# Two-layer transformer on one core: another order for row 3's band values, the first expert blocks and the fetched results in the last stage

## The chip, the cores and the metric

The kernel runs as one program on 1 core of one Trainium2 chip. The metric is the device time of that core in microseconds (us). TensorE is called PE (and PEld for its weight loads), VectorE DVE, ScalarE ACT, GpSimd POOL and SyncE SP. Each engine works through a queue of its own in order; a semaphore holds an engine at an instruction until what it needs is there.

## The reference

There are 4 rows of 512 tokens with 128 channels, all in float32. Each of two layers adds an attention and an expert layer to its input, both reading the same layer norm:

```
x = x + attn0(norm(x)) + experts0(norm(x))   # band attention, 16 heads, window 64; 16 experts, top 4
xn = norm(x)
x = x + attn1(xn) + experts1(xn)             # full attention, 16 heads of 8; 8 experts, top 2

# attn0: logits of the window's 64 pairs from two gelu forms of disp_win - disp;
#        weights = softmax(logits); out = weights @ val_win; out @ W_cproj
# attn1: softmax(q k^T / sqrt(128)) v, then @ w_out
# experts1: score = relu(x rw1 + rb1) rw2 + rb2; gate = softmax over the two best
#        out = sum over experts of gate_e * (relu(x W1_e + b1_e) W2_e + b2_e),  128 -> 512 -> 128
```

The change touches the end of `attn0` for the last row and everything of layer 1.

## The kernel before, in words

**Two stages.** Layer 0 takes the rows one after the other and lasts to about 845 us of the span. The last stage, from there to the end, weaves two tracks: the whole attention of layer 1, and everything else that is left. `weave` and `woven` take at each turn a step from the track whose next step, as a share of the number given with it, is least. A generator's `yield` ends one turn. This decides the order in which the program is written; a scheduler then places each instruction in its engine's queue, with waits as the data needs them. Instructions under `tc.high_priority(offset=FIRST)`, the attention's scores, maxima, exponentials and products, are placed ahead of others.

**Attention.** `full_attention` works on 16 groups (4 rows by 4 groups of 4 heads) in 128 steps. Each step has 8 score matmuls as the profile counts them (L1205). In the first 6 steps both halves serve row maxima (`nmax`, DVE, L1222), in the following 116 one half serves maxima and one exponentials (`ex`, ACT, L1229), since the maxima run 12 pairs ahead, and in the last 6 both serve exponentials. Between steps PE does `weigh` (the products with the values, L1117), `queries` and `keys`, and `columns` (transposes, L1053) into the only buffer of `abank`. `with_maxima` turns a group's maxima and adds them to the queries (`qa`, DVE, L1108); the exponentials' scores of that group need it. `normalise` turns a group's sums and divides (`rd` and `o`, DVE, L1131 and L1132). `turned` (L1141), `project_out` (L1147) and `add_rows` (L287) end a row, and `done` writes the row to the output once attention and experts have both added to it.

**Row 3's band values.** The last row's `attn0` is not yet ended when the last stage begins. ACT makes the weights e (L850), which go to memory as `by_t`. `band_values` then goes through four tiles of tokens: load `f` from `by_t` (L317), turn it on PE (L326) and copy it on ACT (L327) to `g`, store that as `by_s`, load it back with a slant as `wb`, and multiply with the values (L358). `begin` follows (layer norm, `xs`, the router), then `in_order_of_experts`, which sorts the tokens into blocks of one expert each. All this is the generator `row3`.

**Experts.** Blocks hold 128 pairs of a token and its expert. `early` has the 31 blocks of rows 0 to 2, `last_row` the 15 of row 3. `experts(m, pool, deep)` fetches the weights `wx` and rows `xb` by indirect DMA on POOL (L581), turns the rows (L604, copied at L606), and multiplies twice: the first half L637 with its four activations (three on ACT at L650, one on DVE at L648), the second half L611 with its bias on DVE (`y`, L618) and the store to `ys` (SP, L619). The halves' PSUM comes from `bank`, which has two buffers; `y` has one. `paced` keeps the halves in their place between the attention's steps.

**Results.** `results(m, lag)` fetches, a round, two tiles' rows of `ys` (`got`, four fetches on POOL) and adds the fetched rows with their gates to x, `lag` rounds later (L676, DVE). `behind` ties the first of a round's fetches to the attention's pace, and with lag over 1 also the first sum of each even tile.

**The last stage's second track.** Before, `row3` and the first 36 turns of the early experts are woven, then come the rest of the early experts, then `results(early, 2)` woven with the last row's experts, and then `results(last_row, 1)`.

Of the kernel before, what the change touches and what calls it, by code (L numbers as in the profile page):

```python
# [30 lines left out]
B, T, C = 4, 512, 128  # L31
# [66 lines left out]
def woven(*tracks):  # L98


    live = [[g, n, 0] for g, n in tracks]
    while live:
        t = min(live, key=lambda v: (v[2] + 1) / v[1])
        t[2] += 1
        if next(t[0], "end") == "end" or t[2] == t[1]:
            live.remove(t)
        yield


def weave(*tracks):  # L110
    for _ in woven(*tracks):
        pass
# [3 lines left out]
def two_layers(ctx: ExitStack, tc: tile.TileContext, w: dict, consts: bass.AP, out: bass.AP):  # L116
# [8 lines left out]
    def bank():  # L125
        return ps_f.tile([P, 512], FP, tag="f", name="bank")
# [17 lines left out]
    def c_(name):  # L144
        return cst[:, offs[name][0]:offs[name][1]]
# [92 lines left out]
    def transposed(src):  # L238

        pt = bank()  # L240
        for i in range(TPB):
            nc.tensor.transpose(pt[:, i * P:(i + 1) * P], src[:, i, :], ident)
        return pt
# [46 lines left out]
    chain = ctx.enter_context(tc.tile_pool(name="chain", bufs=2))  # L290
# [130 lines left out]
    early, last_row = Pairs(range(B - 1)), Pairs(range(B - 1, B))  # L421
# [11 lines left out]
    def begin(b, pool, tag):  # L433

        m = part_of[b]
        at = (b - m.rows[0]) * TPB
        own = slice(at, at + TPB)
        xn = chain.tile([P, TPB, C], FP, tag="o", name="xn", bufs=1)
        rw1 = pool.tile([C, F1], FP, tag=tag, name="rw1")
        nc.sync.dma_start(out=rw1, in_=w["L1_ffn_rw1"])  # L440
        layernorm(b, xn)
        nc.sync.dma_start(
            out=m.xs[at * P:(at + TPB) * P, :].rearrange("(t p) c -> p t c", p=P), in_=xn
        )
        yield
        pt = transposed(xn)
        nc.scalar.copy(xT[:, b * T:(b + 1) * T], pt)
        yield
        hs = []
        for c in range(4):  # L450
            ph = bank()
            paced(nc.tensor.matmul(ph, rw1[:, c * P:(c + 1) * P], xT[:, b * T:(b + 1) * T], start=True, stop=True))
            h = chain.tile([P, T], FP, tag="h", name="h", bufs=4)
            nc.scalar.activation(h, ph, AF.Relu, bias=cols[:, c:c + 1])
            hs.append(h)
            if c % 2:
                yield
        pg = bank()
        for i in range(TPB):
            for c in range(4):  # L460
                nc.tensor.matmul(
                    pg[:, i * E1:(i + 1) * E1], hs[c][:, i * P:(i + 1) * P], rw2[:, c, :],
                    start=(c == 0), stop=(c == 3),
                )
        scores = small.tile([P, TPB, E1], FP, tag="scores1", name="scores1")
        nc.vector.tensor_tensor(
            scores, pg[:, :TPB * E1].rearrange("p (t e) -> p t e", e=E1),
            rb2[:, None, :].to_broadcast([P, TPB, E1]), ALU.add,
        )
        routes(  # L470
            small, "pairs", scores, E1, K1, c_("lead8"), m.gates[:, own, :], m.picks[:, own, :]
        )
        yield
# [111 lines left out]
    def experts(m, pool, deep):  # L585

        NS, NB, xs, ys = m.tiles, m.blocks, m.xs, m.ys
        wx, xb, xbT = {}, {}, {}

        def weights(j):  # L590
            wx[j] = pool.tile([P, WX], FP, tag="wx", name="wx", bufs=deep)
            fetch(wx[j], w["pair_weights"], m.which[:, j:j + 1])

        def load(g):
            k = min(2, NB - 2 * g)
            xb[g] = pool.tile([P, 2, C], FP, tag="xb", name="xb", bufs=2)
            for i in range(k):
                fetch(xb[g][:, i, :], xs[:, :], m.whose[:, 2 * g + i:2 * g + i + 1])

        def turn(g):  # L600
            k = min(2, NB - 2 * g)
            pt = bank()
            for i in range(k):
                nc.tensor.transpose(pt[:, i * P:(i + 1) * P], xb[g][:, i, :], ident)  # L604
            xbT[g] = pool.tile([C, 2 * P], FP, tag="xbT", name="xbT", bufs=2)
            nc.scalar.copy(xbT[g][:, 0:k * P], pt[:, 0:k * P])  # L606

        def second(j, h):
            py = bank()
            for c in range(4):  # L610
                mm = nc.tensor.matmul(  # L611
                    py[:, 0:C], h[:, c * P:(c + 1) * P], wx[j][:, F1 + c * P:F1 + (c + 1) * P],
                    start=(c == 0), stop=(c == 3),
                )
                own = own + [mm] if c else [mm]
            paced(own[0], own[-1])
            y = pool.tile([P, C], FP, tag="y", name="y")
            nc.vector.tensor_tensor(y, py[:, 0:C], wx[j][:, 2 * F1 + 4:WX], ALU.add)  # L618
            nc.sync.dma_start(out=ys[j * P:(j + 1) * P, :], in_=y)  # L619

        for j in range(deep):
            weights(j)
        load(0)
        yield
        load(1)
        turn(0)
        yield
        late = None
        for j in range(NB):
            g = j // 2  # L630
            if j % 2 and 2 * (g + 1) < NB:
                turn(g + 1)
                if 2 * (g + 2) < NB:
                    load(g + 2)
            ph = bank()
            for c in range(4):
                mm = nc.tensor.matmul(  # L637
                    ph[:, c * P:(c + 1) * P], wx[j][:, c * P:(c + 1) * P],
                    xbT[g][:, j % 2 * P:(j % 2 + 1) * P], start=True, stop=True,
                )  # L640
                own = own + [mm] if c else [mm]
            paced(own[0], own[-1])
            h = pool.tile([P, T], FP, tag="h", name="h", bufs=2)
            for c in range(4):
                b1 = wx[j][:, 2 * F1 + c:2 * F1 + c + 1]
                to = h[:, c * P:(c + 1) * P]
                if c == 3:
                    nc.vector.tensor_scalar(to, ph[:, c * P:(c + 1) * P], b1, 0.0, ALU.add, ALU.max)  # L648
                else:
                    nc.scalar.activation(to, ph[:, c * P:(c + 1) * P], AF.Relu, bias=b1)  # L650
            yield
            if late:
                second(*late)
            late = (j, h)
            if j and j - 1 + deep < NB:
                weights(j - 1 + deep)
            yield
        second(*late)
        yield

    def results(m, lag):

        got = {}
        for g in range(m.tiles // 2 + lag):
            if g < m.tiles // 2:
                got[g] = chain.tile([P, 2, 2, C], FP, tag="h", name="got", bufs=4)
                for i in range(2):
                    for k in range(2):
                        ins = fetch(got[g][:, i, k, :], m.ys[:, :], m.place[:, k, 2 * g + i:2 * g + i + 1])
                        if not i and not k:  # L670
                            behind(ins)
            if g >= lag:
                for t in range(2 * (g - lag), 2 * (g - lag) + 2):
                    x = x1[:, m.rows[0] * TPB + t, :]
                    for k in range(2):
                        ins = nc.vector.scalar_tensor_tensor(  # L676
                            x, got[g - lag][:, t % 2, k, :], m.gate[:, k, t:t + 1], x, ALU.mult, ALU.add
                        )
                        if not t % 2 and not k and lag > 1:
                            behind(ins)  # L680
                    if t % TPB == TPB - 1:
                        done(m.rows[0] + t // TPB)
            yield

    def after(*parts):
        for p in parts:
            yield from p


    with ExitStack() as l0:  # L690
        prep = l0.enter_context(tc.tile_pool(name="prep", bufs=1))
# [32 lines left out]
        ready = {}  # L724
# [237 lines left out]
        pq = l0.enter_context(tc.tile_pool(name="begin0", bufs=1))  # L962
# [67 lines left out]
    def full_attention():  # L1030
# [163 lines left out]
        for t in range(min(todo), max(todo) + 1):  # L1194
# [37 lines left out]
            yield  # L1232

    pq = ctx1.enter_context(tc.tile_pool(name="experts", bufs=1))
    first_experts = experts(early, pq, 3)
    row3 = after(band_values(B - 1, ready[B - 1][1]), begin(B - 1, chain, "valn"), in_order_of_experts(last_row, pq, pq, "tb"))
    weave(
        (full_attention(), 142),
        (after(
            woven((row3, 32), (first_experts, 36)), first_experts,  # L1240
            woven((results(early, 2), 9), (experts(last_row, pq, 3), 34)), results(last_row, 1),
        ), 32 + 66 + 9 + 34 + 3 + 10),
    )


# [40 lines left out]
```

## Time and profile before

| | us |
|---|---|
| median of three timed runs | 1317.91 |
| lowest and highest of them | 1314.45 and 1323.61 |
| the profiled execution's own time | 1310.25 |
| its span, first to last instruction | 1308.1 |
| busy in the span: PE, DVE, ACT, POOL | 1027.7, 1010.7, 955.3, 139.1 |
| start of attention step 1, 6, 119 | 870.5, 891.35, 1269.55 |
| DVE's sums L676 waiting for `got`, 15 times in all | 27.8 |
| PE's L326 waiting for `f`, once | 16.8 |
| mean granted clock of PE | 0.903 |

The profile is of one execution. In its rows the start or the busy time comes first, then the mean length of one, engine and line of the kernel, the operation with its output and input, and in brackets the idle time before it and what ended that. A busy share over the whole span mixes layer 0, which lives on DVE and ACT, with the last stage, which lives on PE. So the last stage is read from views cut to its own stretch of time.

### The profile page before, as it was taken

Reading aid. Unit: us, or ns where it says so; the run is one execution under the profiler, and the core shown is the slowest. Engines: PE = TensorE matmul, PEld = TensorE weight load, DVE = VectorE, ACT = ScalarE, POOL = GpSimd, SP = SyncE. Lnnn points to the kernel's source line nnn. Section 1 sums busy time; section 2 is a strip of 40 time slices with the busy share of each in tenths; the row PEclk is TensorE's granted clock in tenths of the full one; section 3 lists DMA queues with packets and bytes.
Section 4 is the critical chain, followed back from the end, with each engine's and each line's share of the span. In section 5 each row is a group of like instructions: output and inputs, shape, how many; then the busy total and the mean of one; then the engine's idle time right before and its main releaser. Section 6 shows DMA issues by size and latency. Waiting matters only on the chain. (4 is left out here: it accounts for less than half of the span.)

```text
span 1308.1 us, 18393 instructions
## 1 busy us (share of the span) xinstructions
PE 1027.7 (79%) x7029; PEld 463.6 (35%) x7029; DVE 1010.7 (77%) x1246; ACT 955.3 (73%) x1154; POOL 139.1 (11%) x165
## 2 busy tenths in 40 slices
PE   5677876778796677897577886739898999978996
PEld 3232333223342132443222342414344545534442
DVE  5999999999988999998999979625355475545552
ACT  5999998999987899898899987224454445534454
POOL 3000000000000000000000000231121123234512
PEclk9898898889998799898788988759999999989999
DMA  7221213347212445311355411154632324532431
GB/s 272 65 85 43 73 55 131 84 117 181 57 46 79 116 105 144 99 57 32 123 131 143 122 51 29 63 164 124 169 93 94 97 66 123 144 104 90 122 112 37
DMA packets 161969, 132.17 MB, mean 101 GB/s; under 512 B 68101, under 2 KB 142266, under 8 KB 160346
## 3 DMA queue, kind: packets, MB, share of 16 engines
q1 hardware_dynamic: 151290, 91.72, 25.7%
q0 software_dynamic: 10304, 38.64, 9.5%
q8 instruction: 56, 0.92, 0.3%
q10 hardware_dynamic: 288, 0.64, 0.1%
q14 instruction: 31, 0.25, 0.1%
HBM read 97.93 MB, written 33.03 MB: 100 GB/s over the span
## 5 line engine op out<-in xcount | busy, mean ns | idle before, releaser
L790 DVE TENSOR_TENSOR z<-proj 128x2044 f32<-128x2044 f32 (+31 forms) x256 | 547.8, 2161 | 14.3 <-PE lbank L804 10.1
L804 PE MATMUL lbank<-z,place 128*32 128x504 f32 (+18 forms) x2048 | 302.5, 669 | 135.2 <-ACT z L796 73.4
L796 ACT ACTIVATE z<-z,posb 128x1024 f32<-128x1024 f32 (+31 forms) x256 | 264.3, 1100 | 24.3 <-DVE z L790 23.6
L792 ACT ACTIVATE z<-z,brep 128x2048 f32<-128x2048 f32 (+31 forms) x128 | 240.8, 1913 | 13.7 <-DVE z L790 11.2
L1229 ACT ACTIVATE ex<-score 128x1024 f32<-128x1024 f32 x128 | 130.4, 1024 | 160.7 <-PE score L1205 160.7
L1222 DVE TENSOR_REDUCE nmax<-score 128x2 f32<-128x1024 f32 x128 | 156.1, 1224 | 84.6 <-PE score L1205 84.2
L804 PEld LDWEIGHTS lbank<-z,place 128*32 128x32 f32 x2048 | 45.3, 115 | 288.9 <-ACT z L796 150.7
L1205 PE MATMUL score<-kpad,qpad 32*128 32x512 f32 x384 | 111.4, 652 | 19.4 <-DVE nmax L1222 14.1
L581 POOL DMA_INDIRECT wx<-pair_weights,which x46 | 43.5, 946 | 663.9 <-PE abank L1097 432.4
L1205 PE MATMUL score<-qa,kpad 32*128 32x512 f32 x384 | 104.1, 654 | 2.9 <-ACT ex L1229 2.8
L893 PE MATMUL accbank<-wT,lin 128*128 128x128 f32 x512 | 84.8, 308 | 23.7 <-DVE lin L891 23.6
L893 PEld LDWEIGHTS accbank<-wT,lin 128*128 128x128 f32 x512 | 71.9, 210 | 75.3 <-DVE lin L891 39.1
L906 PE MATMUL gbank<-tT,wT 128*128 128x512 f32 x128 | 73.3, 656 | 27.1 <-DMA wT<-wT_all 21.2
L648 DVE TENSOR_SCALAR h<-bank,wx 128x128 f32<-128x128 f32 x46 | 16.0, 349 | 77.9 <-ACT h L650 77.9
L913 PE MATMUL gbank<-tT,wT 128*128 128x512 f32 x128 | 69.3, 624 | 4.5 <-ACT glu L909 4.5
L1117 PE MATMUL accbank<-ex,vaug 128*32 128x512 f32 x512 | 71.1, 621 | 0.2 <-ACT ex L1229 0.2
L650 ACT ACTIVATE h<-bank,wx 128x128 f32<-128x128 f32 x138 | 40.7, 365 | 39.2 <-PE bank L637 39.1
L637 PE MATMUL bank<-xbT,wx 128*128 128x128 f32 x368 | 53.9, 291 | 4.3 <-DVE y L618 3.5
L637 PEld LDWEIGHTS bank<-xbT,wx 128*128 128x128 f32 x368 | 47.4, 201 | 24.3 <-issue 15.1
L611 PEld LDWEIGHTS bank<-wx,h 128*128 128x128 f32 x368 | 46.6, 197 | 21.5 <-issue 19.0
L611 PE MATMUL bank<-wx,h 128*128 128x128 f32 x368 | 53.4, 289 | 0.8 <-ACT g L327 0.6
L909 ACT ACTIVATE glu<-gbank,gbt 128x512 f32<-128x512 f32 x64 | 44.2, 690 | 9.0 <-PE gbank L906 6.4
(242 smaller groups left out, 1379.8 us busy)
## 6 DMA issues: line engine op xcount, KB each, us to landing
r<-route SPq DMA_DIRECT2D x64, 256.0 KB
wb<-by_s SPq DMA_DIRECT2D x32, 512.0 KB
wT<-wT_all SPq DMA_DIRECT2D x48, 192.0 KB
by_t<-e SPq DMA_DIRECT2D x8, 1024.0 KB
f<-by_t SPq DMA_DIRECT2D x128, 64.0 KB
by_s<-g SPq DMA_DIRECT2D x16, 512.0 KB
wb<-by_s SPq DMA_DIRECT2D x24, 256.0 KB
by_s<-zero POOLq DMA_DIRECT2D x4, 1024.0 KB, 11.0
```

What stands on the lines that cost most here:

```text
L611: mm = nc.tensor.matmul(py[:, 0:C], h[:, c * P:(c + 1) * P], wx[j][:, F1 + c * P:F1 + (c + 1) * P], start=(c == 0), stop=(c == 3),)
L637: mm = nc.tensor.matmul(ph[:, c * P:(c + 1) * P], wx[j][:, c * P:(c + 1) * P], xbT[g][:, j % 2 * P:(j % 2 + 1) * P], start=True, stop=True,)
L790: nc.vector.tensor_tensor(z[:, :, :, 0:n], seen, own, ALU.subtract)
L792: nc.scalar.activation(z[:, :, :, 0:n], z[:, :, :, 0:n], AF.Gelu, bias=b_dmg)
L796: last = nc.scalar.activation(z[:, dq, :, 0:n], z[:, dq, :, 0:n], AF.Gelu, bias=posb[:, j:j + 1])
L804: mm = nc.tensor.matmul(ps[q:q + 32, t0:T], place[:, kind, 3 - dd:35 - dd], z[:, dq, hg, 0:n], start=(dd == 0), stop=(dd == 3),)
L893: nc.tensor.matmul(ya[:, i * P:(i + 1) * P], lin[:, i * P:(i + 1) * P], wT[:, 2, :], start=False, stop=(e == E0 - 1 and i == TPB - 1),)
L906: nc.tensor.matmul(pg, wT[:, 0, :], tT, start=True, stop=True)
L1117: mm = nc.tensor.matmul(av[n][r:r + 32, :], vaug[b % 2][:, i, g * 4 + h, :], ex[n, i][:, h, :], start=(i == 0), stop=(i == TPB - 1),)
L1205: mm = nc.tensor.matmul(ps[:, h - two, :], own[r, i * P:(i + 1) * P], seen[r, :], start=True, stop=True)
L1222: freed.append(nc.vector.tensor_reduce(nmax[n % 2][:, i, two:two + 2, 8:9], ps, AX.X, ALU.max, negate=True))
L1229: freed.append(nc.scalar.activation(ex[n, i][:, two:two + 2, :], ps, AF.Exp, scale=inv))
```

## The change

`row3` takes its first turn (the loads of its first `f`) before the weaving begins. A helper `some(g, n)` gives n turns of a generator. The early experts take 8 turns before `row3` goes on; the remaining 31 turns of `row3` are then woven with 30 of the early experts (31 and 30 in place of 32 and 36). After the early experts' end the last row's experts take 5 turns alone, and only then are the results of rows 0 to 2 woven in, with a lag of three rounds in place of two. The last row's experts are made together with the early ones. The track's length, which `weave` goes by, is given as 157 in place of 154. The number of every kind of instruction stays as it was.

```diff
+    def some(g, n):
+
+        for _ in range(n):
+            next(g)
+            yield
+
...
     pq = ctx1.enter_context(tc.tile_pool(name="experts", bufs=1))
-    first_experts = experts(early, pq, 3)
-    row3 = after(band_values(B - 1, ready[B - 1][1]), begin(B - 1, chain, "valn"), in_order_of_experts(last_row, pq, pq, "tb"))
+    row3 = after(
+        band_values(B - 1, ready[B - 1][1]), begin(B - 1, chain, "valn"), in_order_of_experts(last_row, pq, pq, "tb")
+    )
+    first_experts, last_experts = experts(early, pq, 3), experts(last_row, pq, 3)
+    next(row3)
     weave(
         (full_attention(), 142),
         (after(
-            woven((row3, 32), (first_experts, 36)), first_experts,
-            woven((results(early, 2), 9), (experts(last_row, pq, 3), 34)), results(last_row, 1),
-        ), 32 + 66 + 9 + 34 + 3 + 10),
+            some(first_experts, 8), woven((row3, 31), (first_experts, 30)), first_experts,
+            some(last_experts, 5), woven((results(early, 3), 9), (last_experts, 29)), results(last_row, 1),
+        ), 8 + 61 + 28 + 5 + 38 + 3 + 14),
     )
```

## The prediction, made before the changed kernel ran

> **What bounds the kernel now.** I read first the busy rows of the page, then the busy time by windows of 30 us over the second layer, then the timeline of the places where TensorE stands, and last the chain of work that ended last. Over the whole span no engine is full, and that average hides two regimes:
>
> ```profile
> PE 1027.7 (79%) x7029; PEld 463.6 (35%) x7029; DVE 1010.7 (77%) x1246; ACT 955.3 (73%) x1154; POOL 139.1 (11%) x165
> ```
>
> Up to about 845 us VectorE and ScalarE carry layer 0. Until that boundary the two kernels' instruction orders are equal on every engine, so only the last 465 us can move. The windows (start and end, length, busy PE, PEld, DVE, ACT, POOL, granted clock, DMA share, GB/s) show that PE is nearly full there (26.91 of 30), with two holes, at 850 and near 1165:
>
> ```profile
> 850.00:880.00 30.00, 10.05 (x60) 5.43 (x58) 4.97 (x5) 7.42 (x9) 12.76 (x10) 0.56 0.55 165
> ...
> 1150.00:1180.00 30.00, 21.48 (x143) 9.16 (x144) 12.89 (x18) 11.00 (x17) 10.63 (x12) 0.89 0.31 87
> 1240.00:1270.00 30.00, 26.91 (x209) 13.90 (x205) 17.35 (x28) 15.89 (x29) 6.78 (x7) 1.00 0.38 111
> ```
>
> PE is fed in attention steps (0 to 127, counted by the L1205 scores). A step with little else takes 2.54 us: scores 1.14, then the row maxima (1.23) or the exponentials (1.02). The first hole, in the timeline:
>
> ```profile
> 851.75 3.71 ACT L850 ACTIVATE e<-e 128x2048 f32<-128x2048 f32 x2
> ...
> 859.98 6.97 SPq L317 DMA_DIRECT2D f<-by_t  x11
> ...
> 867.09 1.94 PE L326 MATMUL bank<-cst,f 128*128 128x128 f32 x8 [16.84 <-DMA f<-by_t]
> ...
> 870.47 1.14 PE L1205 MATMUL score<-k,q 32*128 32x512 f32 x8
> ```
>
> PE's queue is in order. The transposes of row 3's band weights (L326) stand ahead of step 1, so PE waits 16.84 us for a round trip: e on ACT, to memory, back as f. The second hole and the end come below.
>
> **The change part by part.** Nothing is added or removed; the counts of every instruction agree. Things move.
>
> *Opening.* After, eight turns of the first experts and steps 1 to 4 stand ahead of L326; f's loads are still issued first. PE runs its first block half (L637) at about 851 and then needs a PSUM bank that ACT frees only behind the two e exponentials (851.75 + 3.71 = 855.46), three L650 (0.89) and a copy (0.37): 856.7. Another half (1.69 at half clock) puts step 1 at about 858.5, against 870.47. Steps 1 to 5 then take 3.6 to 4.5 each (two maxima 2.36 plus scores 1.14 at full or 2.09 at half clock), so step 6 starts at 876 to 880, against 891.35: 11 to 16 us earlier, and I take **−14**. f landed at 867; L326 comes at about 870, so its wait is hidden. Were it not, each us of lateness would cost one. One more weight fetch now queues on POOL behind fills until about 864; its block is due later.
>
> *Packing.* In the new order I gave each step from 6 to 120 the larger of 2.54 and 1.15 plus the PE work put into it (block half 1.1, L1117 1.0, L1053 0.2 each). The sum is 342.5 before and 346.4 after: block halves leave the late steps, which have room, for steps that have none. **+4** (between +2 and +6).
>
> *Row 3's chain.* f to g to the store of by_s to its reload to L358: the trace has 4.09 us of waiting at the reload of the third tile, and its two steps lose 6.3. After, that tile has four steps between stages instead of two, which spares 4 to 6; the second has only four and SP's queue holds the q and k round trip ahead of its store, estimated at +2. **−3** (−6 to +2).
>
> *Sums of rows 0 to 2.* The first group of fetched results is the second hole:
>
> ```profile
> 1166.38 0.35 DVE L676 SCALAR_TENSOR_TENSOR x<-got,gate,x 128x128 f32<-128x128 f32 x1 [5.83 <-DMA got<-ys,place]
> ...
> 1169.25 1.22 PE L1205 MATMUL score<-kpad,qpad 32*128 32x512 f32 x2 [6.82 <-DVE nmax L1222]
> ```
>
> DVE's sum waits for the fetch with the maxima behind it, and PE waits for these: step 87 took 8.55 instead of 2.54 and step 88 5.27, about 8.1 lost; three later groups lost 0.65, 1.3 and 2.6, in all 12.65. One round more of lag defers only the even tiles' sums, which `behind` paces anyway; an odd tile's sums stand where the schedule expected the data. In the new order the first comes two steps after the last block's y (L618): a wait of 4.9 and 2 for the cold clock, then 2.9, 1.4 and 1.25: 12.4. **0** (−5 to +4).
>
> *The end*, where the change works against itself. Before:
>
> ```profile
> 1272.21 1.14 PE score L1205 x8
> ...
> 1282.74 1.10 PE bank L611 x8
> 1283.85 0.02 issue
> 1283.87 0.30 DVE y L618
> 1284.17 0.02 issue
> 1284.19 3.32 DMA ys<-y
> ...
> 1304.05 0.69 DVE x L287
> ```
>
> The chain that ended last runs from the last row's last block through ys and eight fetches 1.25 apart into the output; meanwhile the attention ran on freely, because `qa` of the last group stood ahead of all last-row sums on DVE. After, the last two block halves (L611) stand together behind step 119, and the sums of the last row are interleaved with what attention needs. From step 119's start (before 1269.55, called T):
> - y is one buffer: the second L618 waits for the first's store (T+2.6 to T+5.9), with step 120's maxima behind it: y at T+6.2, step 121 at T+7.5 instead of T+5.2.
> - Its store lands at T+9.5; fetches are issued at T+10.4, 11.7 and 12.9, and land 2.5 later. DVE's next entries are two L676 needing the second and third fetch: done at T+15.9. Behind them are `rd` and `o` of group 14 (0.55), which release the one `abank` that PE's L1053 ahead of step 122 wants: step 122 at T+16.8, before T+7.7.
> - The fourth fetch waits for L1117 of step 122, T+19.1 at full clock. The fourth to seventh land until T+25.6, four L676 stand before `qa`, and step 124 waits for `qa`: T+27, before T+14.3. That is 12.7 later.
> - From step 124 to the end took 24.3; 1.3 of that was `rd` and `o` held behind the last L676, which goes: **+11.4**.
>
> The clock is where the trace and the Trainium skill differ. Here PE came out of the 6.82 us wait at half rate (1.22 for a pair of score matmuls that took 0.70 before it) and was back at 1174.5, 5.3 us later; and a gap of only 2.41 us, ending at 1213.2, was followed by a block half of 2.08 instead of 1.16. The page "TensorE: Matmul & The Clock Gate", section "HAM oscillation", warns of idle gaps over about 3.4 us only. By the rule the 2.1 us gap before step 121 is harmless, and both say that the 7 us before step 122 are not; what the rule leaves open is how soon full rate is back. Taken as harmless throughout, as in the steps above, the clock adds nothing: +11.4. By the trace, step 122's scores and products at half rate delay the fourth fetch by 1.8, and the two slow steps after 124 add about 1: +14.2. I lean to the trace: **+13** (+5, if DVE's waits overlap better than I see, to +16).
>
> Sum: −14 + 4 − 3 + 0 + 13 = **0** on the profiled execution's 1310.25 (span 1308.1 and 2.15 around it). The median of the three timed runs is 7.66 higher, 1317.91; the sum carries over: **1318 us**.
>
> **The rivals.** A timed comparison of this kernel tells about 1% (13 us) from no change.
> - *Likeliest: the opening's gain is given back at the end.* 1318, own range 1306 to 1330. For it: both are read from queue orders. Chance 0.50.
> - *The end does not bite.* If the fetches' landings overlap the tail so that `qa` comes only 5 us late, and reload and sums reach their better ends: −14 + 4 − 6 − 5 + 5 = −16, or 1302; with the best of opening and packing, 1298. For it: ACT and PE have slack in the tail. Against it: a DVE queue cannot overtake. Chance 0.25.
> - *Sums of rows 0 to 2 stall more often.* The place is L676 of the odd tiles; the price 8.1 each as at 1166; from three full stalls it decides: 3 × 8.1 + 2.6 = 26.9, 14 over before, so 1332; four would give 1340. For it: fetches start only when the last ys store lands and the lag does not pace odd tiles. Against it: only the first of six groups cost that much. Chance 0.25.
> - *The shift does nothing*, because another wait (the e exponentials, or f) holds PE until 867 all the same: then +14 in place of 0, within the third's time. I leave it little: the experts' rows and weights were in place before 850.
>
> The range runs from 1298, the best of the second case, to 1336, between the third's three and four stalls; about 0.15 is left out, most of it above.
>
> **What would show it.** Right: the 16.84 us wait at L326 gone, step 1 near 858 and step 6 near 878; PE busy in 850 to 880 from 10 to about 20; step 119 some 13 earlier than 1269.6; then two PE gaps, each over 5 us, before steps 122 and 124, `qa` behind four L676, and the end about 51 after step 119 instead of 38.5. Wrong: steps 119 to end within 42 us (second case); several L676 waits above 4 us with score waits behind them (third case); PE idle past 862 in the opening (fourth).

## The result, and the profile after

The changed kernel takes **1332.13 us** (median of six runs, 1327.55 to 1337.24); the kernel before, run beside it, 1317.26 (six runs, 1314.45 to 1323.61). The ratio is 1.0107, with a 95% interval of 1.0067 to 1.0146: slower, by about one per cent. The profiled execution took 1327.55, its span 1325.7 (before 1308.1). The six executions of each kernel lie 9 to 10 us apart and both profiles are of short ones, so differences of profiles and of medians need not agree to the microsecond.

The page's busy row says that the engines do the same work as before:

```profile
PE 1032.5 (78%) x7029; PEld 463.9 (35%) x7029; DVE 1011.7 (76%) x1246; ACT 955.4 (72%) x1154; POOL 139.4 (11%) x165
```

PE is busy 4.8 us longer at the same count; so most of the answer lies in waits. Lines behind 688 have moved: the scores are L1211 now (before L1205), the maxima L1228, `qa` L1114, the products L1123, the transposes into `abank` L1059, `rd` and `o` L1137 and L1138. The windows that answer to the two holes of before, and the last stretch, in the same columns (busy PE, PEld, DVE, ACT, POOL, granted clock, DMA share, GB/s):

```profile
850.00:880.00 30.00, 18.70 (x114) 12.05 (x114) 15.25 (x17) 9.61 (x17) 19.88 (x18) 0.83 0.50 158
...
1150.00:1180.00 30.00, 23.03 (x164) 10.52 (x162) 13.99 (x20) 11.96 (x20) 9.15 (x10) 0.94 0.36 97
...
1270.00:1308.00 38.00, 25.10 (x153) 8.15 (x146) 11.93 (x24) 13.78 (x18) 7.57 (x8) 0.82 0.10 27
```

The first hole is filled in part (18.70 of 30 where 10.05 was); the second is still there; and the last stretch, whose clock was 0.94, has 0.82 and goes on for another 18 us. Cut at the starts of attention steps, from the timeline of both kernels:

| stretch (us) | before | after | difference | predicted |
|---|---|---|---|---|
| start to step 0 (layer 0, same order) | 840.8 | 843.8 | +3.1 | 0 |
| step 0 to 6, the opening | 50.6 | 36.4 | −14.1 | −14 |
| step 6 to 85 | 264.3 | 275.8 | +11.5 | +1 (packing +4, chain −3) |
| step 85 to 119, with the sums of rows 0 to 2 | 113.9 | 119.3 | +5.3 | 0 |
| step 119 to the end | 38.6 | 50.4 | +11.8 | +13 |
| span | 1308.1 | 1325.7 | +17.6 | 0 |

**The opening.** In the timeline PE now has work in the hole, and f is turned four steps later (behind step 4 in place of step 0), without a wait for it:

```profile
853.33 2.08 PE L637 MATMUL bank<-xbT,wx 128*128 128x128 f32 x8 [0.25 <-ACT xbT L606]
...
859.39 2.07 PE L637 MATMUL bank<-xbT,wx 128*128 128x128 f32 x8 [3.55 <-ACT xbT L606]
861.39 1.90 PE L1211 MATMUL score<-k,q 32*128 32x512 f32 x8
...
874.15 0.60 PE L326 MATMUL bank<-cst,f 128*128 128x128 f32 x4
```

**Steps 6 to 85.** PE waits for the reload of the band tiles. The third tile, in the timeline (SPq rows are the issues of transfers):

```profile
943.29 0.55 SPq L332 DMA_DIRECT2D by_s<-g  x1
...
946.84 2.31 SPq L344 DMA_DIRECT2D wb<-by_s  x3
...
949.24 2.31 SPq L619 DMA_DIRECT2D ys<-y  x1
951.34 0.43 PE L358 MATMUL bank<-wb,va 128*32 128x128 f32 x8 [3.56 <-DMA wb<-by_s]
...
952.60 0.36 SPq L344 DMA_DIRECT2D wb<-by_s  x1
...
954.50 0.63 PE L358 MATMUL bank<-wb,va 128*32 128x128 f32 x2 [1.94 <-DMA wb<-by_s]
...
955.06 1.22 PE L1211 MATMUL score<-kpad,qpad 32*128 32x512 f32 x2
```

From the store's issue to the first product 8.05 us pass; PE had only 4.5 us of other work for them. The last of the four reloads is issued behind a store of `ys` on SP's queue. And then the scores run at half rate (1.22 instead of 0.70).

**The sums of rows 0 to 2.** The row that answers to the 6.82 us stall is two steps earlier and a little shorter:

```profile
1162.06 0.35 DVE L676 SCALAR_TENSOR_TENSOR x<-got,gate,x 128x128 f32<-128x128 f32 x1 [6.12 <-DMA got<-ys,place]
...
1163.69 1.22 PE L1211 MATMUL score<-kpad,qpad 32*128 32x512 f32 x2 [5.16 <-DVE nmax L1228]
```

**The end.** Step 119 starts at 1275.36:

```profile
1279.75 0.29 DVE L618 TENSOR_TENSOR y<-bank,wx 128x128 f32<-128x128 f32 x1 [1.68 <-DMA ys<-y]
...
1287.72 0.35 DVE L676 SCALAR_TENSOR_TENSOR x<-got,gate,x 128x128 f32<-128x128 f32 x1 [0.86 <-DMA got<-ys,place]
1287.99 0.25 DVE L1137 RECIPROCAL rd<-abank 128x16 f32<-128x16 f32 x1
1288.28 0.29 DVE L1138 TENSOR_TENSOR o<-abank,rd 128x128 f32<-128x128 f32 x1
...
1288.71 0.45 PE L1059 MATMUL abank<-cst,nmax 128*128 128x128 f32 x1 [5.89 <-DVE o L1138]
...
1289.09 2.09 PE L1211 MATMUL score<-qa,kpad 32*128 32x512 f32 x8
...
1293.35 0.94 POOL L581 DMA_INDIRECT got<-ys,place  x1 [7.28 <-PE accbank L1123]
...
1293.36 1.14 PE L1211 MATMUL score<-qa,kpad 32*128 32x512 f32 x8
...
1299.65 0.35 DVE L676 SCALAR_TENSOR_TENSOR x<-got,gate,x 128x128 f32<-128x128 f32 x1 [0.92 <-DMA got<-ys,place]
1299.92 0.68 DVE L1114 TENSOR_TENSOR qa<-abank,qpad 128x512 f32<-128x512 f32 x1
...
1300.75 2.09 PE L1211 MATMUL score<-qa,kpad 32*128 32x512 f32 x8 [4.99 <-DVE qa L1114]
```

DVE's in-order queue carries the wait across: a sum that needs a fetch stands ahead of `o`, and `o` stands ahead of step 122; four more stand ahead of `qa`, and `qa` ahead of step 124. The chain of work that ended last, which before ran along the last block's y and its fetches, now runs through these sums and `qa`.

### The profile page after: what moved, and what is told of

Read it like the earlier page. It is cut to its first block, busy times and chain, and to the rows that moved or that the text cites. A ratio compares the mean times of both kernels' runs of the same rounds, so it can differ in the third digit from the quotient of the medians.

```text
span 1325.7 us, 18390 instructions
## 1 busy us (share of the span) xinstructions
PE 1032.5 (78%) x7029; PEld 463.9 (35%) x7029; DVE 1011.7 (76%) x1246; ACT 955.4 (72%) x1154; POOL 139.4 (11%) x165
## 5 line engine op out<-in xcount | busy, mean ns | idle before, releaser
L798 ACT ACTIVATE z<-z,brep 128x2048 f32<-128x2048 f32 (+31 forms) x128 | 240.6, 1911 | 15.9 <-DVE z L796 13.4
L1228 DVE TENSOR_REDUCE nmax<-score 128x2 f32<-128x1024 f32 x128 | 156.1, 1223 | 83.7 <-PE score L1211 82.3
L1211 PE MATMUL score<-kpad,qpad 32*128 32x512 f32 x384 | 113.0, 662 | 22.8 <-DVE nmax L1228 16.0
L1211 PE MATMUL score<-qa,kpad 32*128 32x512 f32 x384 | 108.0, 690 | 6.7 <-DVE qa L1114 5.0
L1123 PE MATMUL accbank<-ex,vaug 128*32 128x512 f32 x512 | 73.6, 642 | 0.2 <-ACT ex L1235 0.2
L650 ACT ACTIVATE h<-bank,wx 128x128 f32<-128x128 f32 x138 | 40.7, 366 | 37.1 <-PE bank L637 28.8
L611 PEld LDWEIGHTS bank<-wx,h 128*128 128x128 f32 x368 | 46.9, 199 | 23.1 <-issue 18.8
L637 PEld LDWEIGHTS bank<-xbT,wx 128*128 128x128 f32 x368 | 46.6, 198 | 23.3 <-issue 11.8
```

The lines of the kernel that those rows point to most:

```text
L611: mm = nc.tensor.matmul(py[:, 0:C], h[:, c * P:(c + 1) * P], wx[j][:, F1 + c * P:F1 + (c + 1) * P], start=(c == 0), stop=(c == 3),)
L637: mm = nc.tensor.matmul(ph[:, c * P:(c + 1) * P], wx[j][:, c * P:(c + 1) * P], xbT[g][:, j % 2 * P:(j % 2 + 1) * P], start=True, stop=True,)
L798: nc.scalar.activation(z[:, :, :, 0:n], z[:, :, :, 0:n], AF.Gelu, bias=b_dmg)
L1123: mm = nc.tensor.matmul(av[n][r:r + 32, :], vaug[b % 2][:, i, g * 4 + h, :], ex[n, i][:, h, :], start=(i == 0), stop=(i == TPB - 1),)
L1211: mm = nc.tensor.matmul(ps[:, h - two, :], own[r, i * P:(i + 1) * P], seen[r, :], start=True, stop=True)
L1228: freed.append(nc.vector.tensor_reduce(nmax[n % 2][:, i, two:two + 2, 8:9], ps, AX.X, ALU.max, negate=True))
```

## The experiments

All are compared with the kernel before, run beside them (1316.2 to 1316.4 in the three groups of runs). The stretches come from one profiled execution each, cut as above:

| kernel | time, us | ratio (95%) | 0 to 6 | 6 to 85 | 85 to 119 | 119 to end |
|---|---|---|---|---|---|---|
| before | 1317.3 | 1.0 | 50.6 | 264.3 | 113.9 | 38.6 |
| changed | 1332.1 | 1.0107 (1.0067–1.0146) | 36.4 | 275.8 | 119.3 | 50.4 |
| e1, row 3's shift alone | 1314.9 | 1.0001 (0.9966–1.0036) | 35.5 | 272.3 | 121.1 | 39.9 |
| e2, results part alone | 1323.2 | 1.0051 (1.0026–1.0075) | 50.9 | 268.8 | 121.4 | 41.7 |
| e3, last row's sums tied | 1313.3 | 0.9977 (0.9953–1.0001) | 36.5 | 270.9 | 124.2 | 40.6 |
| e6, all sums tied | 1307.4 | 0.9930 (0.9912–0.9948) | 37.3 | 266.4 | 115.7 | 40.0 |
| f5, row 3 woven wider | 1314.2 | 0.9984 (0.9963–1.0006) | 37.9 | 257.0 | 122.8 | 50.5 |
| f9, pace 153 | 1320.6 | 1.0028 (0.9995–1.0061) | 35.6 | 270.3 | 125.3 | 40.7 |
| f7, all sums tied, no shift | 1328.3 | 1.0094 (1.0056–1.0133) | 50.3 | 275.8 | 117.4 | 39.2 |
| f8, before with ties | 1319.5 | 1.0016 (0.9997–1.0036) | 50.3 | 269.6 | 121.2 | 37.8 |
| g1, e6 and wider | 1306.2 | 0.9910 (0.9881–0.9939) | 35.6 | 269.2 | 115.7 | 39.5 |
| g2, e3 and wider | 1314.8 | 0.9987 (0.9961–1.0014) | 35.7 | 269.9 | 127.1 | 40.4 |
| g3, before, wider | 1312.3 | 0.9966 (0.9940–0.9991) | 41.8 | 268.1 | 119.3 | 39.0 |

**The change's two parts, one at a time.** First the shift of row 3 with the results left alone, on the changed kernel:

```diff
-            some(last_experts, 5), woven((results(early, 3), 9), (last_experts, 29)), results(last_row, 1),
-        ), 8 + 61 + 28 + 5 + 38 + 3 + 14),
+            woven((results(early, 2), 9), (last_experts, 34)), results(last_row, 1),
+        ), 8 + 61 + 28 + 9 + 34 + 3 + 10),
```

> The shift of row 3 alone; the results part as before (woven in from the start of the last row's experts, lag 2, track length 153, which is the pace of before). Theory (the profile after: opening -14, stretch of steps 6 to 85 +11.5, sums of rows 0 to 2 +5, end +12): the opening's gain and the loss in steps 6 to 85 both stay, the sums and the end are as before, because DVE's order there is that of before (qa of the last group ahead of all last-row sums): 1314 to 1319 us, ratio about 0.998; step 119 to the end about 38.5 us. Rival (the shift of row 3 also brings the late end, because everything behind it comes earlier): 1328 or more, step 119 to the end near 50 us.

Measured: 1.0001 and an end of 39.9 us. The shift by itself neither gains nor loses, and it does not bring the late end. Steps 85 to 119, which should have stayed as before, took 7.2 more. Then the results part alone, on the kernel before:

```diff
-            woven((results(early, 2), 9), (experts(last_row, pq, 3), 34)), results(last_row, 1),
-        ), 32 + 66 + 9 + 34 + 3 + 10),
+            some(last_experts, 5), woven((results(early, 3), 9), (last_experts, 29)), results(last_row, 1),
+        ), 32 + 66 + 5 + 38 + 3 + 14),
```

> The results part alone; row 3 and the first experts as before. Theory: no gain in the opening (16.8 us wait at L326 as before), steps 6 to 85 as before within 3 us, sums of rows 0 to 2 about 5 us dearer; in this order DVE has qa ahead of the last-row sums and rd and o of group 14 ahead of them too, so the end costs at most 3 us more: in all +5 to +9, about 1324 us, ratio 1.004 to 1.007. Rival (the longer lag and later start by themselves make the late end): +16 or more, 1333 us, step 119 to the end near 50 us.

Measured: 1323.2, as the theory had it; the end costs 3.1 more, steps 85 to 119 7.5 and steps 6 to 85, which I had held to 3, 4.5. The two parts together would be worth +0.5%; the change has +1.1%, and the three intervals together just leave room for no difference. What the profiles show to be missing is the end, which neither part has: the order on DVE that makes it arises only where both meet. The track length was not the same in the three (153, 158 and 157); what it does alone comes with f9 below.

**Is the end DVE's order?** On the changed kernel every sum of the last row is tied to the attention's pace, two rounds later; the track length grows by the two turns that this adds:

```diff
-                        if not t % 2 and not k and lag > 1:
+                        if m is last_row or not t % 2 and not k and lag > 1:
                             behind(ins)
...
-            ... results(last_row, 1),
-        ), 8 + 61 + 28 + 5 + 38 + 3 + 14),
+            ... results(last_row, 3),
+        ), 8 + 61 + 28 + 5 + 38 + 5 + 14),
```

> The changed kernel with the last row's sums tied to the attention's pace (lag 3 for the last row, every sum of it tied; two turns more), so that qa and rd and o of the attention stand ahead of them on DVE. Theory (DVE's order makes the end): the two PE gaps ahead of steps 122 and 124 go, step 119 to the end falls from 50.3 to 37 to 40 us, time 11 to 13 us less than the changed kernel: about 1320 us, ratio 1.002. Rival (the end is long because the last blocks' store and fetches land late): the waits move to the sums themselves and the end stays at 47 us or more, 1330 us.

Measured: the end is 40.6 us, and the kernel 0.9977, 18.8 us under the changed one by the medians. In the profiles the end is 9.8 us shorter and steps 6 to 85, which the edit was not meant to touch, 4.9, while steps 85 to 119 are 4.9 longer; the spans differ by 7.3 only, since e3's profile is of one of its longer executions (1320.5). What the end is worth is thus shown, the rest of the 18.8 is not located. A second way to the same order is the pace alone:

```diff
-        ), 8 + 61 + 28 + 5 + 38 + 3 + 14),
+        ), 8 + 61 + 28 + 5 + 38 + 3 + 10),
```

> The changed kernel with a track length of 153 in place of 157, nothing else: the second track then ends 3 to 4 attention steps later, and in DVE's order qa comes ahead of all last-row sums, as before. Theory (the end is long because of that order, which the pace alone decides; the longer lag has no part in it): step 119 to the end 38 to 41 us in place of 50.4, time 10 to 12 less than the changed kernel, about 1320 us, ratio 1.001. Rival (lag 3 and the five turns ahead of the results make the loss): no more than 4 us less, ratio 1.008 or more.

Measured: end 40.7, time 1320.6, both as the theory said. One number, the declared length of a track, moves `qa` ahead of the last row's sums. The longer lag alone does not make the late end: f9 still has it.

**The sums of rows 0 to 2.** On the kernel with the last row tied, all other sums are tied as well (`if lag > 1: behind(ins)`):

> As the kernel before it in this list, and every sum of rows 0 to 2 tied to the pace as well, not only the first of each even tile; their first comes about 15 steps later on DVE. Theory (DVE's sums of odd tiles stand ahead of maxima and wait for the fetch): the waits of L676 for got fall from about 32 us to under 10, and steps 85 to 119 lose the 5 us of the change and most of the 12.65 that the kernel before lost: 12 to 16 us less than the kernel without this, about 1305 us, ratio 0.99. Rival (those steps are bound by PE's work or by the experts' own waits): no more than 4 us less, 1316 us or more.

Measured: 1307.4, 5.9 under e3, between theory and rival. No wait of DVE is put down to `got` any more, and steps 85 to 119 fall from 124.2 to 115.7 (PE's waits of the scores for maxima there from 20.7 to 5.8). At the end, where in the changed kernel four sums stood ahead of `qa`, the timeline of this kernel has:

```profile
1277.30 0.69 DVE L1114 TENSOR_TENSOR qa<-abank,qpad 128x512 f32<-128x512 f32 x1 [0.42 <-PE abank L1059]
...
1284.30 1.14 DVE L676 SCALAR_TENSOR_TENSOR x<-got,gate,x 128x128 f32<-128x128 f32 x4 [6.31 <-remote]
...
1285.28 1.14 PE L1211 MATMUL score<-qa,kpad 32*128 32x512 f32 x8 [2.73 <-ACT ex L1235]
```

`qa` is done 6 us before the first of the last row's sums, so DVE's wait of 6.31 holds no scores up. The same ties on the kernel before (lag 2, and lag 3 for the last row):

> The kernel before with only the sums' ties: lag 2 as it was, but every sum of rows 0 to 2 tied to the pace, and the last row's sums tied with lag 3. Theory (the 6.82 us stall at step 88 and the three after it come from untied odd tiles): L676 waits for got fall from 28 to under 10, steps 85 to 119 from 113.9 to about 105, time 5 to 9 less than before, ratio 0.994. Rival (steps 85 to 119 are filled with expert halves, so a stall only moves): ratio 0.998 to 1.001.

Measured: 1.0016, the rival. The waits for `got` went, and others came. In the timeline of this kernel:

```profile
1220.59 0.35 DVE L648 TENSOR_SCALAR h<-bank,wx 128x128 f32<-128x128 f32 x1 [4.52 <-ACT h L650]
1220.86 1.22 DVE L1222 TENSOR_REDUCE nmax<-score 128x2 f32<-128x1024 f32 x1
...
1222.22 1.22 PE L1205 MATMUL score<-kpad,qpad 32*128 32x512 f32 x2 [5.18 <-DVE nmax L1222]
```

Now an expert's activation holds the maxima up. ACT's part of it (L650) waited itself, for something that the trace calls remote. POOL's queue has fetches of `got` among those of weights and rows in these steps, but which of them it was is not settled.

**Steps 6 to 85.** Row 3's turns get more turns of experts between them, on the changed kernel:

```diff
-            some(first_experts, 8), woven((row3, 31), (first_experts, 30)), first_experts,
+            some(first_experts, 8), woven((row3, 31), (first_experts, 44)), first_experts,
...
-        ), 8 + 61 + 28 + 5 + 38 + 3 + 14),
+        ), 8 + 75 + 14 + 5 + 38 + 3 + 14),
```

> The changed kernel with row 3's 31 turns woven with 44 turns of the early experts in place of 30 (the rest of them then 14 in place of 28; track length as before the edit): four to six steps lie between the transposes of a tile (L326) and its products (L358) in place of three to five; the end of the kernel keeps its order. Theory (part of the loss in steps 6 to 85 is the band tiles' round trip through memory, which the change made tighter): PE's and PEld's waits at L358 for wb fall from 21 us to under 10, steps 6 to 85 from 275.8 to about 270, time 1326 us, ratio 1.006. Rival (those steps are filled, and the waits only show where the filling is missing): steps 6 to 85 stay within 3 us of 275.8, ratio 1.010.

Measured: 1314.2, better than the theory. The two rows of the list of waits for L358 in the changed kernel (total, times, longest) are

```profile
PEld bank L358 <- DMA wb<-by_s: 11.9, 6, 4.4
...
PE bank L358 <- DMA wb<-by_s: 9.4, 5, 3.6
```

and in this one there is one row:

```profile
PEld bank L358 <- DMA wb<-by_s: 0.8, 1, 0.8
```

(A weight load and its product wait through the same time, so the two rows are not to be added.) Steps 6 to 85 fall by 18.8 us, twice the 9.4 that PE waited: PE's idle time there falls by 8.8 and its busy time by 10.0, and all but some 2 us of the latter is the same work done faster (the records hold one block half and two of the 512-wide products less); the granted clock over these steps is 0.99 in place of 0.96. The windows show it, first the changed kernel,

```profile
920.00:960.00 40.00, 31.16 (x306) 16.01 (x305) 14.12 (x19) 13.85 (x22) 4.74 (x5) 0.87 0.56 146
```

then this one:

```profile
920.00:960.00 40.00, 36.24 (x328) 18.66 (x328) 20.86 (x29) 20.18 (x33) 7.56 (x8) 1.00 0.65 171
```

The edit moved other waits too: those for `o` and `qa` fall from 5.7 to 0.4, those for the maxima rise from 4.9 to 10.2. So the reload is the largest wait that goes, but not the only thing that changed. The same width on the other kernels:

> The kernel with all sums tied to the pace and row 3 woven with 44 turns instead of 30 (both edits on the changed kernel). Theory (the body's loss is the band tiles' crowding, the end's loss DVE's order; the two are independent and add): steps 0 to 6 near 37, 6 to 85 near 258, 85 to 119 near 116, the end 40: 8 us less than with the ties alone, 1299 us, ratio 0.987. Rival (what the wider weave spares comes back as work in steps 85 to 119): 1306 us or more, ratio 0.992.

> The changed kernel with row 3 woven with 44 turns and only the last row's sums tied. Theory: against the wider weave alone (1314) the end gives 10 back: 1304 us, ratio 0.990; against the kernel with all sums tied it tells what the ties of rows 0 to 2 are worth, 3 to 6 us. Rival (the ties of rows 0 to 2 carry nothing, as they carried nothing on the kernel before): within 2 us of that kernel.

Measured: 1306.2 and 1314.8. The first has the rival's time, but not its cause: steps 85 to 119 stay at 115.7, as the theory said. The second fits neither: it lies 10.8 over the theory and 8.6 over g1, where the rival had 2 at most. In both it is steps 6 to 85 that were wrong: they took 269.2 and 269.9, not 258, and PE waits 5.8 and 7.3 us at L358 again. In the order of both, the third tile's transposes are spread over steps 25 to 27 and its products begin at step 29, where f5 has 27 and 31. So the width is not what decides; where each stage falls between two steps does, and a shift of one turn elsewhere moves it. (e3 has the reverse: the last of that tile's transposes stand one step earlier than in the changed kernel, behind 22, with the products behind 25 as there, and the wait is 0.95 in place of 5.5.) The ties of rows 0 to 2 are worth 8.6 us here (steps 85 to 119: 127.1 against 115.7), against my 3 to 6. On the kernel before, with 52 turns in place of 36:

> The kernel before with one number changed: row 3's 32 turns woven with 52 turns of the early experts instead of 36. L326 of the first tile then stands behind step 3 instead of ahead of step 1, without the change's turn ahead and without its eight first turns; the results part and the end are those of before. Theory (the opening's wait and the crowding of the band tiles are what the shift is about, and the weave's width alone mends both): steps 0 to 6 about 39 in place of 50.6, steps 6 to 85 about 258 in place of 264, the end 38.5: 1300 us, ratio 0.987. Rival (f's loads, now behind 3 us of other issues, land later and PE waits for them behind step 3): no more than 8 us less than before, ratio 0.994 or more.

Measured: 1312.3, the rival's side, though not by its cause: behind step 3 PE did not wait for f. L326 went there, and the opening took 41.8 in place of 50.6, but steps 6 to 85 took 3.8 more than before and steps 85 to 119 5.4 more.

**What the shift is worth.** The kernel with all ties, with row 3 put back:

> The kernel with all sums tied to the pace, its row 3 and first experts put back as they were before (32 turns woven with 36, no first turn ahead). Theory (the shift of row 3 gains 14 in the opening and gives 8 to 11 of it back until step 85): 3 to 7 us more than with the shift, about 1313 us, ratio 0.997. Rival (the loss until step 85 belongs to the faster pace, not to the shift, which then is worth its whole 14): 1320 us or more, ratio 1.003.

Measured: 1328.3, on the rival's side. Between the medians of e6 and this kernel lie 20.9 us, more than the opening (13.0). The two profiles do not locate the rest. Steps 6 to 85 are 9.4 longer here, but 7.0 of that is busy time at a lower granted clock (0.94 against 0.97), and layer 0, the same work in the same order, is 13.4 shorter. That the shift gives back what it gains, as in e1, is by the times no property of the shift.

**The changed kernel a second time:**

> The changed kernel once more, for a second profile of it. If its losses lie in the order of its instructions, the same places recur: steps 0 to 6 near 36.4, steps 6 to 85 near 276 with 15 to 25 us of waits at L358 for wb, step 119 to the end near 50 with the two PE gaps of over 5 us ahead of steps 122 and 124. If they were chance of one execution, steps 6 to 85 differ by over 5 us.

Measured: 1339.2. The waits at L358 recur in the list of waits,

```profile
PEld bank L358 <- DMA wb<-by_s: 15.2, 6, 4.3
PE bank L358 <- DMA wb<-by_s: 12.5, 5, 4.1
```

and so do the opening (36.3), the end (48.7) and its two gaps (5.91 and 4.49). Steps 6 to 85 took 283.8, 8.0 more than in the first profile and so beyond the 5 that I had set for chance: a single execution tells that stretch only to some 8 us, and the smaller differences in the table above are to be read so. Of the 8.0 only 1.4 is idle time; 6.6 is PE's busy time for the same matmuls, at a granted clock of 0.93 in place of 0.96. The order of instructions sets the places of the waits and, within some 2 us, their sum (PE waits 11.2 and 12.9 us for the reload, 3.5 and 3.5 for `o`, 2.2 and 2.2 for `qa`); the clock between them varies.

## Why the prediction was right or wrong

The sum came out at 0, with the range 1298 to 1336 around it; the measurement is 1332, a slowdown of about 15 us. The range held it, in part by luck: its upper end came from a case that did not happen, and two stretches came out above the ranges of their terms. The likeliest case, a standstill at 1306 to 1330, did not come. Its mechanism did: the opening gained 14 and the end lost 12. The sum missed by what lies between them. Step 119 came 5.8 later than before, not 13 earlier.

- **The opening was right** to the microsecond: −14.1. PE's two block halves at half rate and the wait for ACT's copy (3.55) are the steps that I named; step 1 came at 861.4, 17.5 us behind step 0. L326's wait is gone and no long one took its place.
- **The end was right in mechanism and size**: +11.8 against +13, and f9 and e3 show that it is DVE's order. Single terms differ: the store of the first y took 1.68 us of waiting, not 3.3, so step 121 was late by under 1 us and not by 2.3. Step 122 started 13.7 us behind step 119, not 16.8. The clock behaved as in the profile of before: step 122 ran at half rate (2.09) behind a gap of 5.89, and its products (L1123, 1.94) delayed the fourth fetch; steps 124 and 125 were slow too.
- **The step that failed is the one from 6 to 85: "Row 3's chain", −3, with "Packing", +4**: together +1, measured +11.5. PE's idle time rose by 11.9 in these steps at nearly the same busy time (0.3 less). Of this 5.4 is the reload (L358 and L362, from 5.8 to 11.2), where I had said less waiting. I counted the steps between a tile's stages, not the time. The third tile's transposes stand behind steps 21 to 23 and its products behind 25 and 26, where they stood behind 19 and behind 21 to 23; but the steps between are short ones: behind its last transpose and ahead of the wait lie 5.5 us of other work after (942.28 to 951.34, less 3.56) and 6.5 before (935.28 to 945.86, less 4.09). I named only the q and k round trip ahead of a store on SP; stores of `ys` and loads of the next f stand there too (a load of f held SP for 4.14 us, and the first tile's reload was issued 6.7 us behind its store instead of 3.6). The rest is waits that "Packing" put at nothing, since it gave each step only its own PE work: for `o` (0.9 to 3.5), `qa` (none to 2.2) and ACT's copy `xbT` (0.2 to 1.7). They recur in the second profile to a tenth. And the reload is not the only way to lose these steps: e1, with the same shift, waits 5.2 for it, no more than before, and its stretch is 8.0 longer all the same, with 10.5 of waits for maxima in place of 5.5.
- **The sums of rows 0 to 2 were set at 0**, and their stretch came to +5.3, over the bound of +4. But the waits that I had counted hardly moved: the scores wait 12.4 for maxima in place of 12.3. The first group lost what I had said (5.16 and the slow step), a later one more (PE waited 3.43 at step 93), others less. What was added is idle time elsewhere, for `qa` (2.1), `ex` (1.3) and `h` (1.2), and 1.5 of busy time; I had not looked there.
- **Layer 0** took 3.1 more in this profile at the same order. In the profiles of the other kernels step 0 starts between 836.5 and 849.8: that is the spread of single executions, and the timed difference of 14.9 between the medians (17.6 between the spans) is consistent with it.

Of the rivals, none came true as told. The third gave nearly the measured time (1332), but for another cause: there was one full stall, not three.

## What to carry to other kernels

In a weave of in-order queues, a wait belongs to whatever stands behind it: before adding work that depends on a transfer, list what the same engine must still do for the critical engine, and tie the new work behind that. The declared pace of a track is part of the order: one number moved 10 us of the end. Measure the room for a round trip through memory in microseconds between its stages, not in loop steps, since a change that makes the steps shorter shrinks that room. And count a stall of PE at more than its length, because steps behind it can run at half clock: in the one pair that shows it here, 9.4 us of waits went with 18.8 us. The best kernels here keep row 3's shift and tie every sum: e6 at 0.9930 and g1 at 0.9910, and between these two the intervals overlap.

## What the hardware showed

In the prediction I took gaps near 2.5 us as enough for half rate. They can be, but the length does not decide. In the profile of before, the block half right behind the gap of 2.41 us still ran at full rate (1.16); the half rate began with the scores behind it and took in the next block half (2.08). The two executions of the changed kernel, with one order of instructions, have nearly the same gap ahead of step 93, first

```profile
1188.94 0.70 PE L1211 MATMUL score<-kpad,qpad 32*128 32x512 f32 x2 [3.43 <-DVE nmax L1228]
```

and then

```profile
1199.33 1.22 PE L1211 MATMUL score<-kpad,qpad 32*128 32x512 f32 x2 [3.37 <-DVE nmax L1228]
```

The longer gap left PE at full rate, the shorter was followed by half rate. It is the same with a later gap ahead of L1153: 2.06 us left the full rate, 2.20 was followed by scores of 1.22. Neither of the two readings that the prediction weighed sorts these four; what does is not settled here. The return takes some time: behind the 5.89 gap PE was at full rate 4.3 us after it began work again (1289.09 to 1293.36), behind the 4.99 gap about 6 us (1300.75 to 1306.85), with a pause of 0.21 between. In f5 only one of the 79 steps from 6 to 84 had slow scores (over 1.6 us for the eight), against two in the changed kernel's first profile and six in its second. This, more than the waits themselves, is how the same order of instructions took 275.8 and 283.8 us for these steps.
